# Sandwich block: expert weights loaded from ACT's queue instead of SP's, and a new order of the steps of an expert pair

## The chip, the cores and the metric

One core of a Trainium2 chip runs the whole kernel. TensorE (PE) multiplies matrices into PSUM; VectorE (DVE), ScalarE (ACT) and GpSimd (POOL) do the rest of the arithmetic; SyncE (SP) computes nothing and issues most of the transfers, which 16 DMA engines carry out. Each engine works through its own instructions in order. The metric is the device time of one execution in microseconds; the time of a kernel is the median of its timed runs.

## The reference

Eight sequences of 512 rows of width 256 (4096 rows, f32) go through two parts. Both are normalised and added back to their input.

- Attention: 16 query heads over 4 key and value groups, width 128, with positions added to queries and keys, causal softmax, and an output projection.
- Experts: a gate picks the best 6 of 64 experts for each row. Each expert takes at most 64 rows (`CAP`), in the order of the rows, and computes `silu(x @ w_gate) * (x @ w_up)` with hidden width 176, then `@ w_down`. The results are weighted by the gate's scores and summed. A shared expert of width 352 is computed for every row.

```python
x = x + layernorm(attention(layernorm(x)))
buf  = rows of layernorm(x) gathered by expert       # 64 experts x 64 places x 256
g, u = silu(buf @ w_gate), buf @ w_up                # 256 -> 176
d    = (g * u) @ w_down                              # 176 -> 256
y    = sum over the 6 chosen of topk_w * d  +  shared expert
x = x + layernorm(y)
```

## The kernel before

**Attention sets the beat.** The main loop (lines 884 to 936) runs over `k`, the 128 pairs of a sequence and a head; here such a pass is called a head. The order of the instructions on every engine is written out by hand: what stands first in the loop is issued first. Head `k` computes `scores(k)` (`psc`, line 280; DVE's minimum, line 284; ACT's exponentials, line 287), `project(k-3)` (`po`, line 352), `queries(k+1)` (`pq`, line 267) and `mix(k-2)` (`pav`, line 340, then ACT's copy `ao`, line 108). The probabilities of head `k-1` are turned on the way: DVE transposes blocks into `eb` (line 313), SP stores them to a DRAM tile (`ex_d`, line 317) and loads them back in four parts as `et` (line 320), which `mix` reads one head later. The four loads wait until the store has landed.

**Experts run beside it.** When five sequences have been routed (`EARLY = 5`), the generator `experts()` (lines 612 to 631) works through 32 pairs of experts, two experts of 64 rows side by side. It is advanced at fixed places of the loop, four times in most heads, and each pair step takes two advances; so most heads hold two steps, one in the middle (line 903) and one at the end (line 934). In step `m` stand, for different pairs:

```python
for behind_, step in ((5, down), (4, turn_hidden), (3, gate_up), (2, turn_rows),
                      (1, load_gate_up), (2, load_down)):
    if 0 <= m - behind_ < NM:
        step(m - behind_)
```

- `start_pair` (line 501): POOL gathers the pair's rows into `gx`.
- `load_gate_up` (line 509): two transfers of 352 KB into `wgu`, two buffers. `load_down` (line 518): one of 352 KB into `wd`, two buffers.
- `turn_rows` (line 525): two PE transposes `ptx` (128x128), DVE's copy `gxt`.
- `gate_up` (line 536): PE's `pgu`, for each of the two experts a product with 64 columns of the array (a column-tiled product: the two experts' outputs lie in the two halves of the PSUM tile), then ACT's tanh `hid` (line 544). DVE makes `hid` of it at the next advance (lines 550 and 551).
- `turn_hidden` (line 553): two PE transposes `pth` (128x88), DVE's copy `ht`.
- `down` (line 562): PE's `pd`, column-tiled in the same way, then two ACT activations `dd` (line 576), and POOL's scatter-add into `y_d` (line 577).

A load has to wait until the products of the pair two before have read its buffer. `load_gate_up(m-1)` stands in the step in which `gate_up(m-3)` frees the buffer. `load_down(m-2)` stands one step ahead of `down(m-4)`, which frees its buffer. All these loads are issued by SP, in one queue with `ex_d` and `et`.

PSUM banks come from three pools; `pq`, `pav`, `pd` and `pgu` take turns in three banks (`ps_m`), `psc`, `pth` and `ptx` in three others (`ps_s`).

At the end, pairs with more rows than fit are done again ("late": lines 915 to 923 and the loop from line 948), through the same loading functions with the key `"late"`.

Of the kernel before, what the change touches and what calls it, by code (L numbers as in the profile page):

```python
# [19 lines left out]
P = 128  # L20
# [10 lines left out]
FC = F // 2  # L31
# [12 lines left out]
def sandwich_kernel(ctx, tc, x, wq, bq_t, wkv, bk_t, bv, wo, gate_wt, w_gate, w_up, w_down,  # L44
                    sh_gate_t, sh_up_t, sh_down_t, pe_t, out):
    nc = tc.nc
# [75 lines left out]
    with ExitStack() as part:  # L122
# [313 lines left out]
        def tables():  # L436


            pm = ps_m.tile([NX, CAP], F32, tag="m", name="pm")
            nc.tensor.matmul(pm, lhsT=ident[:, NX:], rhs=keys[0][:, :CAP], start=True, stop=True)  # L440
            both = p1.tile([NX, 2 * CAP], F32, tag="both", name="both")
            nc.vector.tensor_copy(both[:, :CAP], keys[0][:NX, :CAP])
            nc.vector.tensor_copy(both[:, CAP:], pm)
            first = p1.tile([NX, CAP], F32, tag="first", name="first")
            yield
            for n, _ in enumerate(best(first, both)):
                if n % 2:
                    yield
            pk = ps_m.tile([P, NM], F32, tag="m", name="pslot")
            cols = ident[:NX, :NX].rearrange("p (m k) -> p k m", k=2)  # L450
            for odd in range(2):
                nc.tensor.matmul(pk[ts(odd, CAP), :], lhsT=first, rhs=cols[:, odd, :], start=True, stop=True)
            none = p1.tile([P, NM], F32, tag="none", name="none")
            nc.vector.tensor_scalar(none, pk, 0.0, own, ALU.is_equal, ALU.mult)
            row = p1.tile([P, NM], F32, tag="row", name="row")
            nc.vector.tensor_scalar(row, pk, 0.0, float(ET_ROWS - NT), ALU.is_equal, ALU.mult)
            nc.vector.tensor_sub(row, row, pk)
            idx = p1.tile([P, NM, 2], U32, tag="idx", name="idx")
            nc.vector.tensor_scalar_add(idx[:, :, 0], row, float(NT))
            nc.vector.scalar_tensor_tensor(idx[:, :, 1], row, offs, none, ALU.add, ALU.add)  # L460
            table["idx"], table["first"] = idx, first
# [37 lines left out]
        table, pairs = {}, {}  # L499

        def start_pair(m):

            l = pairs[m] = {"m": m}
            l["gx"] = p3.tile([P, ROW], F32, tag="gx", name=f"gx_{m}", bufs=3)
            nc.gpsimd.indirect_dma_start(
                out=l["gx"], out_offset=None, in_=xg_d[:, :],
                in_offset=bass.IndirectOffsetOnAxis(ap=table["idx"][:, m, 0:1], axis=0))

        def load_gate_up(key):
            l = pairs[key]  # L510
            m = l["m"]

            l["wgu"] = p3.tile([P, 2, 2, 2, F], F32, name=f"wgu_{key}", **l.get("wgu_at", {"tag": "wgu"}))
            for k, w in enumerate((w_gate, w_up)):
                nc.sync.dma_start(out=l["wgu"][:, :, k, :, :].rearrange("p e c f -> p e (c f)"),
                                  in_=w[ds(m * 2, 2)].rearrange("e (p c) f -> p e (c f)", p=P))

        def load_down(key):
            l = pairs[key]
            m = l["m"]  # L520
            l["wd"] = p3.tile([FC, 2, 2, E], F32, name=f"wd_{key}", **l.get("wd_at", {"tag": "wd"}))
            nc.sync.dma_start(out=l["wd"].rearrange("p e c h -> p e (c h)"),
                              in_=w_down[ds(m * 2, 2)].rearrange("e (p c) h -> p e (c h)", p=FC))

        def turn_rows(key):
            l = pairs[key]
# [20 lines left out]
        def gate_up_hidden(key):  # L547
            l = pairs[key]
            pgu = l.pop("pgu")
            nc.vector.scalar_tensor_tensor(l["hid"], l["hid"], 1.0, pgu[:, 0, :], ALU.add, ALU.mult)  # L550
            nc.vector.scalar_tensor_tensor(l["hid"], l["hid"], 0.5, pgu[:, 1, :], ALU.mult, ALU.mult)
# [60 lines left out]
        def experts():  # L612


            yield from tables()
            yield
            yield from free_slots()
            yield
            for m in range(NM + 5):
                if m < NM:  # L620
                    start_pair(m)
                for behind_, step in ((5, down), (4, turn_hidden), (3, gate_up), (2, turn_rows),
                                      (1, load_gate_up), (2, load_down)):
                    if 0 <= m - behind_ < NM:
                        step(m - behind_)
                yield
                if 0 <= m - 3 < NM:
                    gate_up_hidden(m - 3)
                if m == NM + 4:
                    pairs["all"] = True  # L630
                yield
# [243 lines left out]
        queries(0)  # L875
        behind, ahead = {}, iter(())
        routed, zeroing = experts(), zeros()
        twice, finishing = False, False
        FIRST_FREE = (EARLY + 1) * NH + 6
# [4 lines left out]
        for k in range(NK):  # L884
# [30 lines left out]
            if k == FIRST_FREE:  # L915

                work = table["work"]
                table["rest"] = nc.values_load(work[0:1, 0:1], min_val=0, max_val=NM - 1)
                table["m"] = nc.values_load(work[0:1, 1:2], (ET.DVE, ET.SP), min_val=0, max_val=NM - 1)
                pairs["late"] = {"m": table["m"], "wgu_at": {"tag": "wgu_late", "bufs": 1},  # L920
                                 "wd_at": {"tag": "wd_late", "bufs": 1}}
                load_gate_up("late")
                load_down("late")
# [24 lines left out]
        with tc.For_i(0, table["rest"], 1) as n:  # L948
            m = nc.values_load(table["work"][0:1, ds(n + 2, 1)], (ET.DVE, ET.SP), min_val=0, max_val=NM - 1)
            pairs["late"] = {"m": m}  # L950
            load_gate_up("late")
            load_down("late")
            parts, gts = [], []
            for b in range(EARLY, B):
                q, tag = [(p1, "hid"), (p2, "v"), (p2, "v")][b - EARLY]
                xg = q.tile([P, NI, LROW], F32, tag=tag, name=f"rest_xg_{b}")
                nc.sync.dma_start(out=xg, in_=rows_of(lxg_d, b * T - ET_ROWS))
                q, tag = [(p1, "y"), (p2, "x"), (p2, "x")][b - EARLY]
                mark, marked = marks(m, xg[:, :, E:ROW], xg[:, :, ROW:], f"rest_{b}", q, tag)
                parts.append((xg, mark))  # L960
                gts.append(turn_scores(marked, f"rest_{b}", p2, "kt", 5))
            gather("late", parts)
            gate_up("late")
            gate_up_hidden("late")
            turn_hidden("late")
            down("late")
            for b in range(EARLY, B):
                y = p2.tile([P, NI, E], F32, tag="xnt", name=f"rest_y_{b}")
                nc.sync.dma_start(out=y, in_=rows_of(ly_d, b * T - ET_ROWS))
                for i in range(NI):  # L970
                    py = ps_m.tile([P, E], F32, tag="m", name=f"rest_py_{b}_{i}")
                    nc.tensor.matmul(py, lhsT=gts[b - EARLY][:, ts(i, P)], rhs=pairs["late"]["dd"], start=True, stop=True)
                    nc.vector.tensor_add(y[:, i, :], y[:, i, :], py)
                nc.sync.dma_start(out=rows_of(ly_d, b * T - ET_ROWS), in_=y)
                for _ in output(b, y, residual(b, p1, "xn")):
                    pass
# [50 lines left out]
```

## Time and profile before

| What | us |
|---|---|
| median of three timed runs | 1498.71 (1498.46 to 1499.84) |
| the profiled execution, its own time | 1494.35 |
| its span, first to last instruction | 1492.6 |
| PE busy in the span | 1416.8 (95%) |
| DVE busy | 891.6 (60%) |
| ACT busy | 498.0 (33%) |
| POOL busy | 427.8 (29%) |
| the stage in which the expert pairs run | about 995 to 1302 |

"Busy" is time in which an engine works on at least one instruction. PE's matmuls are pipelined, so a busy PE can still be held up between two of them. A float32 matrix product shows as two matmul instructions. The clock that the throttle grants to PE is listed for each stretch of time as a share of full speed. "SPq" in a listing is SP issuing a transfer; the duration there is the time for which the issue holds SP, not the transfer. DMA share is the time that packets took, over 16 engines; packets of two queues that overlap are both counted, so it can pass 1.

### The profile page before, as it was taken

What the parts mean: (1) busy time and instruction counts of PE and PEld (TensorE: products, weight loads), DVE (VectorE), ACT (ScalarE), POOL (GpSimd) and SP (SyncE); (2) the same over time, 40 slices, a digit from 0 to 9 for tenths busy, and PEclk for the clock granted to TensorE, in tenths of its full rate; (3) what the DMA queues carried; (4) which work ended last, traced back from release to release, by engine and by line L of the source; (5) the groups of instructions that cost most, each with busy time, mean ns of one, the idle gap of its engine ahead of it and who ended that gap; (6) DMA issues with size and microseconds to landing.
All of it is one profiled execution on the core that took longest, in us unless ns stands there. A gap on an engine that the chain in (4) does not pass through costs nothing.

```text
span 1492.6 us, 18592 instructions
## 1 busy us (share of the span) xinstructions
PE 1416.8 (95%) x5350; PEld 856.4 (57%) x5350; DVE 891.6 (60%) x3094; ACT 498.0 (33%) x1434; POOL 427.8 (29%) x682
## 2 busy tenths in 40 slices
PE   7999999999999999999999999989899999999894
PEld 3566655666656665666566656655455545565552
DVE  4565576657665676557665766666455445577442
ACT  1333343233332342233323332233323333444322
POOL 1222231124112322123112311135333354534202
PEclk9999999999999999999999999999999999999997
DMA  5764554355544464355435544459888799878611
GB/s 207 222 189 142 153 165 139 106 155 166 146 140 134 146 185 125 120 159 165 139 104 165 161 142 132 137 164 258 232 239 230 199 251 261 214 215 249 191 48 60
DMA packets 159701, 252.02 MB, mean 169 GB/s; under 512 B 16092, under 2 KB 135869, under 8 KB 159341
## 3 DMA queue, kind: packets, MB, share of 16 engines
q1 hardware_dynamic: 153453, 241.37, 54.3%
q0 software_dynamic: 6144, 9.44, 3.2%
q8 instruction: 44, 0.72, 0.2%
q14 instruction: 60, 0.49, 0.1%
HBM read 143.01 MB, written 107.74 MB: 168 GB/s over the span
## 4 chain that ended last, share of the span: by engine, by line
PE 79%; DMA 8%; DVE 7%; ACT 2%; POOL 1%; issue 1%; SPq 1%; ACTq 0%; POOLq 0%; DVEq 0%
PE pav L340 16%; PE psc L280 15%; PE pq L267 13%; PE po L352 12%; PE pk L239 4%; PE pv L250 4%; DMA ex_d<-eb 3%; PE py L684 3%; PE pgu L541 3%; PE psg L671 3%; PE psu L671 2%; DVE eb L313 2%; DMA wgu<-in_w_up 2%; PE pd L567 2%; DMA y<-y_d 1%
## 5 line engine op out<-in xcount | busy, mean ns | idle before, releaser
L297 POOL TENSOR_SCALAR e<-e,recip 128x128 f32<-128x128 f32 x508 | 266.5, 542 | 847.4 <-DVE recip L294 809.8
L287 ACT ACTIVATE e<-e,least 128x128 f32<-128x128 f32 (+3 forms) x512 | 285.9, 559 | 379.4 <-DVE least L284 372.1
L280 PE MATMUL psc<-kt,qt 128*128 128x128 f32 (+3 forms) x1024 | 309.6, 442 | 21.0 <-DVE least L284 9.9
L340 PE MATMUL pav<-et,v 128*128 128x512 f32 (+3 forms) x1024 | 296.9, 433 | 2.6 <-DMA et<-ex_d 1.8
L340 PEld LDWEIGHTS pav<-et,v 128*128 128x128 f32 x1024 | 194.4, 190 | 165.3 <-issue 122.8
L284 DVE CUSTOM_DVE_ANT_0 e<-psc,mask 128x128 f32<-128x128 f32 (+3 forms) x512 | 231.3, 479 | 52.3 <-PE psc L280 46.5
L267 PE MATMUL pq<-xnt,wq_sb 128*128 128x512 f32 x512 | 243.9, 599 | 0.0
L352 PE MATMUL po<-wo_sb,ao 128*128 128x256 f32 x1024 | 243.2, 380 | 0.7 <-ACT ao L108 0.7
L352 PEld LDWEIGHTS po<-wo_sb,ao 128*128 128x128 f32 x1024 | 192.5, 190 | 68.6 <-issue 38.2
L313 DVE STREAM_TRANSPOSE eb<-e 128x128 f32<-128x128 f32 x756 | 227.4, 364 | 0.1
L108 ACT COPY ao<-pav 128x512 f32<-128x512 f32 x128 | 75.0, 586 | 450.7 <-PE pav L340 450.7
L280 PEld LDWEIGHTS psc<-kt,qt 128*128 128x128 f32 x1024 | 164.8, 192 | 103.6 <-DVE least L284 34.0
L270 DVE SCALAR_TENSOR_TENSOR qt<-pq,bq_sb,pe_sb 128x512 f32<-128x512 f32 x128 | 95.7, 747 | 121.3 <-PE pq L267 121.2
L267 PEld LDWEIGHTS pq<-xnt,wq_sb 128*128 128x128 f32 x512 | 97.4, 193 | 70.9 <-issue 65.4
L287 ACT ACTIVATION_READ_ACCUMULATOR e<-e,least 128x1 f32 x512 | 95.8, 187 | 0.0
L294 DVE RECIPROCAL recip<-total 128x4 f32<-128x4 f32 x128 | 22.8, 178 | 119.7 <-ACT e L287 119.7
L577 POOL DMA_INDIRECT y_d<-dd,idx x32 | 51.1, 1597 | 72.8 <-ACT dd L576 48.6
L239 PE MATMUL pk<-xnt,wkv_sb 128*128 128x512 f32 x128 | 61.0, 604 | 0.0
L252 DVE TENSOR_TENSOR v<-pv,bv_sb 128x512 f32<-128x512 f32 x32 | 22.1, 692 | 64.4 <-PE pv L250 64.4
L250 PE MATMUL pv<-wkv_sb,xnt 128*128 128x512 f32 x128 | 59.7, 593 | 0.0
L541 PE MATMUL pgu<-wgu,gxt 128*64 128x352 f32 x256 | 47.6, 493 | 10.3 <-DMA wgu<-in_w_up 8.5
L242 DVE SCALAR_TENSOR_TENSOR kt<-pk,bk_sb,pe_sb 128x512 f32<-128x512 f32 x32 | 24.0, 751 | 50.2 <-PE pk L239 50.2
(191 smaller groups left out, 1090.1 us busy)
## 6 DMA issues: line engine op xcount, KB each, us to landing
ex_d<-eb SPq DMA_DIRECT2D x126, 640.0 KB
et<-ex_d SPq DMA_DIRECT2D x504, 160.0 KB
wgu<-in_w_gate SPq DMA_DIRECT2D x32, 352.0 KB
wgu<-in_w_up SPq DMA_DIRECT2D x32, 352.0 KB
wd<-in_w_down SPq DMA_DIRECT2D x32, 352.0 KB
y<-y_d SPq DMA_DIRECT2D x10, 512.0 KB
x<-in_x SPq DMA_DIRECT2D x8, 512.0 KB
x_d<-x SPq DMA_DIRECT2D x8, 512.0 KB
```

The lines of the kernel that those rows point to most:

```text
L239: nc.tensor.matmul(pk, lhsT=wkv_sb[:, c, g, 0, :], rhs=s["xnt"][:, c, :], start=c == 0, stop=c == NC - 1)
L250: nc.tensor.matmul(pv, lhsT=s["xnt"][:, c, ts(i, P)], rhs=wkv_sb[:, c, :, 1, :], start=c == 0, stop=c == NC - 1)
L267: nc.tensor.matmul(pq, lhsT=wq_sb[:, c, ts(h, D)], rhs=seqs[b]["xnt"][:, c, :], start=c == 0, stop=c == NC - 1)
L270: nc.vector.scalar_tensor_tensor(qt, pq, bq_sb[:, h : h + 1], pe_sb, ALU.add, ALU.add)
L280: nc.tensor.matmul(psc[:, :w], lhsT=l["qt"][:, ts(i, P)], rhs=seqs[b]["kt"][h // QPG][:, :w], start=True, stop=True)
L284: nc.vector.tensor_tensor_reduce(out=e, in0=psc[:, :w], in1=mask[:, T - w :], scale=-1.0 / math.sqrt(D), scalar=BIG, op0=ALU.add, op1=ALU. ...
L287: nc.scalar.activation(e, e, AF.Exp, bias=l["least"][:, i : i + 1], scale=-1.0, accum_out=l["total"][:, i : i + 1])
L297: engine.tensor_scalar(e, e, recip[:, n : n + 1], 1.0, ALU.mult, ALU.mult)
L313: nc.vector.transpose(blocks.rearrange("p c j t -> p j c t"), l["e"][i][:, js[0] * P : (js[-1] + 1) * P].rearrange("p (j c t) -> p j c t", ...
L340: nc.tensor.matmul(pav[:, :, j:, :], lhsT=seqs[b]["v"][:, j, ts(g, D)], rhs=l["et"][:, :, AT[j] : AT[j] + NI - j, :], start=j == 0, stop=j ...
L352: nc.tensor.matmul(po[b][i // 2][:, i % 2, :], lhsT=ao[:, ts(i, P)], rhs=wo_sb[:, h, :], start=h == 0 and i % 2 == 0, stop=h == NH - 1, sk ...
L541: nc.tensor.matmul(pgu[ts(e, CAP)], lhsT=l["gxt"][:, c, ts(e, CAP)], rhs=l["wgu"][:, e, :, c, :], start=c == 0, stop=c == 1)
```

## The change

The three weight loads of a pair are issued by ACT instead of SP, except those with the key `"late"`, which stay on SP. In a step, `gate_up` moves ahead of `turn_hidden`, so that the two column-tiled products `pd` and `pgu` follow each other on PE, and the transposes `pth` and `ptx` follow them. `load_down` moves from two steps behind to three, so that it stands behind `down` of the pair two before, whose activations read that pair's result. Since ACT's instructions stay in the order of the program, the loads of a step stand behind that step's `dd` and tanh.

```diff
         def load_gate_up(key):
-            l = pairs[key]
+            l, queue = pairs[key], nc.sync if key == "late" else nc.scalar
             m = l["m"]
 
             l["wgu"] = p3.tile([P, 2, 2, 2, F], F32, name=f"wgu_{key}", **l.get("wgu_at", {"tag": "wgu"}))
             for k, w in enumerate((w_gate, w_up)):
-                nc.sync.dma_start(out=l["wgu"][:, :, k, :, :].rearrange("p e c f -> p e (c f)"),
-                                  in_=w[ds(m * 2, 2)].rearrange("e (p c) f -> p e (c f)", p=P))
+                queue.dma_start(out=l["wgu"][:, :, k, :, :].rearrange("p e c f -> p e (c f)"),
+                                in_=w[ds(m * 2, 2)].rearrange("e (p c) f -> p e (c f)", p=P))
 
         def load_down(key):
-            l = pairs[key]
+            l, queue = pairs[key], nc.sync if key == "late" else nc.scalar
             m = l["m"]
             l["wd"] = p3.tile([FC, 2, 2, E], F32, name=f"wd_{key}", **l.get("wd_at", {"tag": "wd"}))
-            nc.sync.dma_start(out=l["wd"].rearrange("p e c h -> p e (c h)"),
-                              in_=w_down[ds(m * 2, 2)].rearrange("e (p c) h -> p e (c h)", p=FC))
+            queue.dma_start(out=l["wd"].rearrange("p e c h -> p e (c h)"),
+                            in_=w_down[ds(m * 2, 2)].rearrange("e (p c) h -> p e (c h)", p=FC))
...
-                for behind_, step in ((5, down), (4, turn_hidden), (3, gate_up), (2, turn_rows),
-                                      (1, load_gate_up), (2, load_down)):
+                for behind_, step in ((5, down), (3, gate_up), (4, turn_hidden), (2, turn_rows),
+                                      (1, load_gate_up), (3, load_down)):
```

## The prediction

> **What bounds the kernel now.** First the slices of the page: PE, its granted clock, DMA.
>
> ```profile
> PE   7999999999999999999999999989899999999894
> PEclk9999999999999999999999999999999999999997
> DMA  5764554355544464355435544459888799878611
> ```
>
> PE is full nearly everywhere; around the stage of the expert pairs (slices 27 to 35) it dips while DMA jumps from 4 or 5 to 8 and 9. The change touches that stage alone, so I read it by windows.
>
> ```profile
> 995.00:1302.00 307.00, 291.99 (x1315) 161.35 (x1314) 160.63 (x557) 103.27 (x284) 135.68 (x154) 0.97 0.87 235
> 1224.00:1230.00 6.00, 6.00 (x17) 2.77 (x14) 1.83 (x5) 0.32 (x1) 3.41 (x3) 0.72 0.97 307
> ```
>
> Columns: window, length, busy PE, weight loads, DVE, ACT, POOL, clock, DMA share, GB/s. In 307 us PE is idle for 15.0 us, and the clock falls to 0.72 in some windows. PE's waits in the stage:
>
> ```profile
> PE pgu L541 <- DMA wgu<-in_w_up: 8.5, 5, 2.5
> PE ptx L530 <- DVE st_o L76: 2.4, 1, 2.4
> PE pgu L541 <- ACT dd L576: 1.7, 1, 1.7
> ```
>
> The third is a weight wait too: at 1270.2 ACT's `dd` had begun and frees nothing that `pgu` needs, while the `wgu` transfer issued at 1265.62 was 6 us under way, as long as those in the first row took. So weights cost 8.5 + 1.7 = 10.2 us of idle PE. Why are they late? SP's own waits in the stage, then a stretch of the timeline.
>
> ```profile
> SPq L320 <- DMA ex_d<-eb: 121.6, 17, 13.7
> SPq L522 <- PE pd L567: 59.2, 13, 12.6
> ```
>
> ```profile
> 1247.65 1.78 SPq L320 DMA_DIRECT2D et<-ex_d  x4
> ...
> 1249.53 0.39 SPq L515 DMA_DIRECT2D wgu<-in_w_gate  x1
> ...
> 1249.96 0.47 SPq L515 DMA_DIRECT2D wgu<-in_w_up  x1
> ...
> 1254.83 0.32 SPq L522 DMA_DIRECT2D wd<-in_w_down  x1
> ...
> 1255.25 0.35 SPq L317 DMA_DIRECT2D ex_d<-eb  x1
> ...
> 1255.91 1.40 PE L541 MATMUL pgu<-wgu,gxt 128*64 128x352 f32 x8 [0.73 <-DMA wgu<-in_w_up]
> ...
> 1263.35 1.74 SPq L320 DMA_DIRECT2D et<-ex_d  x4
> ```
>
> The mid-head step's weights go out at 1249.53, behind `et`, which waited for the store `ex_d`; their buffer had been free since that step's `pgu` ended at about 1242.3. They are read at 1255.91: 6 us of lead instead of 13. Then `wd` waits for a `pd` and holds back `ex_d` and the next `et`. The queue's order makes the wait, not the buffers.
>
> [...]
>
> **The change, part by part.** Against the profiled execution's 1494.35 us.
>
> *Weight waits.* Loads issued by ACT stand behind the tanh `hid`, which follows the end of the `pgu` that frees the buffer, so the mid-head pair goes out at about 1242.6 instead of 1249.5. At stake: 10.2 us of idle PE, and the slow clock after it. Lost there is window times (1 - clock): from 1044, 6 x 0.26 = 1.6; from 1074, 6 x 0.20 = 1.2 and 6 x 0.08 = 0.5; from 1224 and from 1272, 1.7 each; 6.6 us. Together 16.8. From below nothing comes back if bytes are the limit. The sections that hold these waits (995 to 1090 and 1205 to 1302, 192 us) move 244 and 242 GB/s at a share of 0.89; 23 us shorter they would need 243 x 192/169 = 276 GB/s, and the best 6 us window has 321 (1134 to 1140). That is close, so I take three quarters: 12.6 us.
>
> *Tiling switches.* One step of a pair on PE:
>
> ```profile
> 1115.43 1.08 PE L567 MATMUL pd<-wd,ht 88*64 88x256 f32 x8
> 1116.44 0.46 PE L558 MATMUL pth<-ident,hid 128*88 128x128 f32 x2
> 1116.83 1.40 PE L541 MATMUL pgu<-wgu,gxt 128*64 128x352 f32 x8
> 1118.16 0.51 PE L530 MATMUL ptx<-ident,gx 128*128 128x128 f32 x2
> 1118.51 2.45 PE L280 MATMUL psc<-kt,qt 128*128 128x128 f32 x8
> ```
>
> From `pd` to `pth` are 1.01 us. The other products give 0.84 ns per column (512 columns start 427 ns apart), so `pd`, with two halves of the array at once, streams 4 x 213 ns = 0.85: 0.16 us goes to the switch. `pgu`: 1.33 - 4 x 0.293 = 0.16. `pth` to `pgu`: 0.39 against two transposes, 0.1 to 0.16 over. Today a step switches four times (before `pd`, `pth`, `pgu`, `ptx`), afterwards twice. Two fewer save between 0.16 and 0.3 us; I take 0.2. Steps 5 to 34 hold both products: 30 x 0.2 = 6.0 us, range 3 to 9. PE is what ends the stage, so this counts in full.
>
> *Issues on ACT.* Each step's three take 0.39 + 0.47 + 0.36 us on SP (medians): 1.22; 32 steps, 39 us on ACT, whose busy time in the stage goes from 103 to 142 of 307. Mid-head, ACT next waits 4.1 us for `pav` (`ao`: 73.0 us in 18 waits): hidden. At the head's end it next waits 0.9 us for the minimum of `e`, then 2.2 us before the third `e` (1267 to 1269): hidden as well. Taken as 0; without cover, 39 us.
>
> *ACT's new waits.* The built program makes every transfer wait for one about eight earlier, which used the same completion semaphore. For ACT these are mostly older weights; the second step of a head, however, waits for that head's `ex_d` and its first `et`. Queued behind are the next head's exponentials, whose reciprocal DVE waits for, and DVE's `qt` is what PE needs. A stall is absorbed up to about 5 us: 2.2 before the third `e`, and 2.7 between `dd` (done 1125.2) and the `pav` (1127.9) that takes its bank. In a short head `ex_d` can go at 1252.6 (the end of `eb`) instead of 1255.25, lands by 1260.7 if it takes 8.1 us as today, and its `et` some 3 us later (estimate from its quarter of 640 KB), when ACT is just there (tanh at 1264.4). Value: 0; bounds 0 and +3 us in each of 17 heads.
>
> *SP, and `wd`.* SP loses the 59.2 us of waiting for `pd`, so `ex_d` and `et` go earlier; PE waits for `et` nowhere in the stage, so 0. `wd` waited for the `down` of the next step anyway in 13 of 32 cases; one step later it still has two steps of lead, the same as `wgu`. 0; bounds 0 to +3.
>
> Sum: -12.6 - 6.0 = -18.6, or 1475.8 us of profiled time. The timed median lies 0.3% above this execution, so I scale: 1498.7 x 1475.8/1494.35 = 1480 us.
>
> **Rivals.**
> *Bandwidth keeps the waits.* For: share 0.87 over the stage, and the late loads follow stretches at 1.05 and over. Against: 11% of the time in those sections is free, and the 1074 window moves 142 GB/s while PE starves, so order, not bytes, is to blame there. Then a quarter or less of the 16.8 comes back: -4 - 6 = -10 or less; 1489, from 1486 to 1495.
> *It does not do what it says.* Switches hide under weight loads that wait anyway, and the weight waits only move to the pair behind: within 3 us, 1496 to 1501.
> *Slower: ACT stalls at its issues.* One place, the second step of a head: ACT waits for `et` of that head. It decides once `et` lands more than 5 us after the tanh. A store takes up to 14 us today (SP's longest wait 13.7); with two queues sharing, `et` could land 8 us late: 3 us in 17 heads, +51 - 18.6 = +32; at 7 us late, +15. From 1503 to 1535. Against: the store no longer stands behind 1 to 2 MB of weights in one queue.
>
> **How the numbers follow.** Weights in time 0.57, bandwidth 0.23, no effect 0.06, ACT stalls 0.14. Likeliest 1480, its own range 1473 to 1486. Below 1473 all of both gains (16.8 + 9) is needed. To leave out no more than 2 in 10 the range reaches over the bandwidth case: 1473 to 1497. 0.2%, or 3 us, is about what a measurement of this kernel can tell from no change: faster 0.80, same 0.06, slower 0.14.
>
> **What would show it.** In the stage, PE's rows for `wgu` fall below 3 us and the windows of clock 0.72 go, but for the one at 1002 (after DVE's `st_o`). SP's row for `pd` is gone. From `pd` to what follows `ptx`, 2.9 us instead of 3.1. The stage lasts about 288 us. ACT shows `wgu` and `wd` issues of 0.3 to 0.5 us behind `hid`. I am wrong if ACT's issues take over 1 us, if the first `e` of heads starts over 3 us after its minimum, or if PE waits for `qt` or for banks that `dd` frees.

## The result, and the profile after

| | median of the runs, us | ratio to before, 95% interval |
|---|---|---|
| before | 1498.80 | |
| changed | 1490.76 | 0.9947 (0.9935 to 0.9959) |
| changed, measured again | 1489.30 | 0.9939 (0.9915 to 0.9963) |

The change makes the kernel about 8 us faster (1498.80 - 1490.76), 0.53%. I had forecast 1480, 18.7 us faster. The direction and the wide range were right; the size was not, and the measured time is that of my rival "bandwidth keeps the waits" (1486 to 1495).

The profiled execution of before (1494.35) lies below the median of its runs and the first one of the changed kernel (1494.10) above its own, so the two spans (1492.6 and 1492.3) don't show the gain, and I use a second profile of the changed kernel (1485.00) beside the first.

First the slices of the changed kernel's page: PE, its clock, DMA. They look much as before; in the stage, DMA stands at 8 and 9.

```profile
PE   7999999999999999999999999988899998898894
PEclk9999999999999999999999999999999999999987
DMA  5764554355544464355435544469998899777511
```

The steps of a pair on PE (start, duration; the changed kernel). From `pd` to what follows `ptx` are 1026.77 - 1024.04 = 2.73 us; before, 1118.51 - 1115.43 = 3.08. `pgu` follows `pd` after 0.91 us; before, `pth` followed it after 1.01.

```profile
1024.04 1.08 PE L567 MATMUL pd<-wd,ht 88*64 88x256 f32 x8
1024.95 1.36 PE L541 MATMUL pgu<-wgu,gxt 128*64 128x352 f32 x8
1026.24 0.46 PE L558 MATMUL pth<-ident,hid 128*88 128x128 f32 x2
1026.54 0.40 PE L530 MATMUL ptx<-ident,gx 128*128 128x128 f32 x2
1026.77 1.88 PE L267 MATMUL pq<-xnt,wq_sb 128*128 128x512 f32 x4
```

PE's waits between 980 and 1310 us (total, times, longest), the changed kernel, first profile:

```profile
PE pd L567 <- DMA wd<-in_w_down: 6.5, 2, 4.4
PE psc L280 <- DVE ht L111: 6.0, 2, 4.4
PE pav L340 <- ACT dd L576: 5.0, 4, 2.8
PE ptx L530 <- DVE mv_o L82: 2.8, 1, 2.8
```

The rows for `wgu` (8.5 and 1.7 us before) are gone, as forecast. Three new ones stand in their place, 17.5 us together: `wd`, which is now late; `ht`, whose copy stands behind DVE's wait for the next sequence's `x` (5.97 us, from SP's store and load of `x`); and a bank that ACT's `dd` frees late. SP's and ACT's waits show more ("..." stands for rows left out). SP:

```profile
SPq L320 <- DMA ex_d<-eb: 118.7, 21, 9.3
...
SPq L317 <- DMA et<-ex_d: 18.5, 5, 6.9
...
SPq L143 <- DMA x_d<-x: 8.3, 1, 8.3
```

ACT, same kernel and window:

```profile
ACT dd L576 <- DMA y_d<-dd,idx: 19.2, 6, 6.2
ACT e L287 <- DMA et<-ex_d: 19.0, 8, 5.5
...
ACT ao L108 <- DMA wgu<-in_w_up: 7.8, 2, 4.0
```

SP no longer waits for `pd` (59.2 us before), but the wait for `ex_d` is not much shorter (129.5 us before in the same window). ACT, which waited for no transfer here before, now waits for the scatter-add that still reads `dd` (19.2 us), and stands at some of its weight issues. The longest such stall:

```profile
1239.75 0.58 ACTq L515 DMA_DIRECT2D wgu<-in_w_up  x1
1245.10 0.32 ACTq L522 DMA_DIRECT2D wd<-in_w_down  x1
1245.52 0.40 ACT L287 ACTIVATE e<-e,least 128x128 f32<-128x128 f32 x1 [5.51 <-DMA et<-ex_d]
```

`hid` had ended at 1240.01 and the issue before at 1240.33; the next went out at 1245.10, and `e`, whose minimum had been ready since 1240.68, was queued behind it. In the trace this issue carries the same semaphore (100) as the first part of `et`, issued at 1236.45, whose last piece landed at 1245.07. Pauses of over 0.3 us ahead of a weight issue add up to 15.9 us in seven places of the first profile and 12.4 in the second. The rows of `ao` are no such stalls, although they name transfers: at 1112.16, for one, the issues were out by 1109.20 and `ao` followed the end of its `pav` at 1112.12.

**A ledger for the stage.** I cut each trace from the first `ptx` of the stage to its last `pd` and split the length in three: PE idle (length minus busy time), slow clock (the sum of length x (1 - clock) over windows of 4 us), and the rest, which is PE's work at full speed. For the kernel before, the window is this (columns as in the prediction); 296.36 - 283.78 = 12.6 us are idle.

```profile
1002.54:1298.90 296.36, 283.78 (x1281) 156.29 (x1281) 155.41 (x537) 97.70 (x270) 129.10 (x144) 0.97 0.87 235
```

And for the second profile of the changed kernel:

```profile
1002.01:1288.76 286.75, 272.38 (x1281) 157.98 (x1281) 154.94 (x532) 98.14 (x270) 124.51 (x140) 0.98 0.91 242
```

| | length | idle | slow clock | work |
|---|---|---|---|---|
| before | 296.4 | 12.6 | 8.5 | 275.3 |
| changed, first profile | 292.9 | 19.5 | 6.8 | 266.5 |
| changed, second profile | 286.8 | 14.4 | 5.1 | 267.3 |

PE has 8 to 9 us less work and loses about as much time as before, or more (21.1 us before, 26.3 and 19.5 after). So the new order gave what it could, and the waits did not go: they changed their names. That is what the experiments had to explain. Two profiles of one kernel differ here by 7 us in what is lost, so single profiles are read for work and for names of waits, and the timed runs for sizes.

**How early the loads go out.** The lead of a load is the time from the end of its issue (of the second transfer for `wgu`) to the start of the product that reads it. Over the 32 pairs, in us:

| | `wgu`, median | shortest | `wd`, median | shortest |
|---|---|---|---|---|
| before | 10.6 | 5.2 | 15.4 | 10.4 |
| changed, first profile | 13.9 | 9.9 | 12.3 | 8.4 |
| changed, second profile | 13.5 | 9.9 | 12.1 | 8.4 |

So the change did give `wgu` the lead that I wanted, and took lead from `wd`. Before, five of the six longest waits for `wgu` had leads of 5.5 to 7.2 us: late issues. The longest wait for `wd` in the changed kernel had a lead of 14.5:

```profile
1020.33 0.43 ACTq L522 DMA_DIRECT2D wd<-in_w_down  x1
...
1035.22 1.97 PE L567 MATMUL pd<-wd,ht 88*64 88x256 f32 x8 [4.41 <-DMA wd<-in_w_down]
```

In the kernel before, a `wgu` transfer of the same size, issued at 1023.02, was in time with a lead of 5.2. So this wait comes neither from a late issue nor from the size of a single transfer alone. The DMA share from 1020.33 to 1035.22 is 1.03, but it was 1.04 in the kernel before from 1023.02 to 1028.60, so the share doesn't tell the two transfers apart. What held this one so long isn't shown.

### The profile page after: what moved, and what is told of

Same layout as the page of the kernel before. It is cut to its first block, busy times and chain, and to the rows that moved or that the text cites. A ratio compares the mean times of both kernels' runs of the same rounds, so it can differ in the third digit from the quotient of the medians.

```text
span 1492.3 us, 18593 instructions
## 1 busy us (share of the span) xinstructions
PE 1409.6 (94%) x5350; PEld 860.8 (58%) x5350; DVE 890.7 (60%) x3094; ACT 499.5 (33%) x1434; POOL 427.4 (29%) x682
## 5 line engine op out<-in xcount | busy, mean ns | idle before, releaser
L297 POOL TENSOR_SCALAR e<-e,recip 128x128 f32<-128x128 f32 x508 | 269.6, 570 | 814.5 <-DVE recip L294 781.6
L267 PE MATMUL pq<-xnt,wq_sb 128*128 128x512 f32 x512 | 240.8, 593 | 0.0
L577 POOL DMA_INDIRECT y_d<-dd,idx x32 | 51.0, 1593 | 108.0 <-DMA y_d<-dd,idx 43.3
L111 DVE COPY ht<-pth 88x256 f32<-88x256 f32 x32 | 13.4, 418 | 69.5 <-PE pth L558 69.4
```

The source lines that it names most:

```text
L267: nc.tensor.matmul(pq, lhsT=wq_sb[:, c, ts(h, D)], rhs=seqs[b]["xnt"][:, c, :], start=c == 0, stop=c == NC - 1)
L297: engine.tensor_scalar(e, e, recip[:, n : n + 1], 1.0, ALU.mult, ALU.mult)
```

## The experiments

Two theories. **Bytes**: the 16 DMA engines are so loaded in the stage that something is always late, whichever queue issues it. **ACT's stalls**: the loads come in time, but ACT waits at its issues and holds back exponentials and banks.

### One part of the change at a time

Only the order of the steps (`b_order`), all loads on SP as before:

```diff
-                for behind_, step in ((5, down), (4, turn_hidden), (3, gate_up), (2, turn_rows),
+                for behind_, step in ((5, down), (3, gate_up), (4, turn_hidden), (2, turn_rows),
                                       (1, load_gate_up), (2, load_down)):
```

> The kernel before with one edit: gate_up stands ahead of turn_hidden; all loads stay on SP and load_down stays two steps behind. It measures the tiling switches alone. In the trace after the change a step goes from pd to what follows ptx in 2.73 us instead of 3.08, 0.35 us less, in 30 steps 10.5 us. Full switch saving (both theories, congestion and ACT stalls): 0.35 x 30 = 10 us faster than before, about 1488; the changed kernel's other part is then worth nothing or less. My recorded 0.2 us a step: 6 us faster, 1493. If the saving is hidden under weight waits: under 3 us, 1496 to 1499.

Measured: 1499.31, ratio 0.9999 (0.9980 to 1.0017). Nothing, and that is the sharpest result of the study. Its ledger: length 300.2, idle 24.1, slow 8.5, work 267.6. The work fell by 7.7 us, and the idle time grew by 11.5. PE's waits of this kernel:

```profile
PE pgu L541 <- DMA wgu<-in_w_up: 21.0, 9, 3.8
PE ptx L530 <- DMA gx<-xg_d,idx: 3.1, 1, 3.1
```

`pgu` now starts 0.91 us after `pd` instead of 1.40 where it needn't wait, but its weights come no sooner: 8.5 + 1.7 = 10.2 us of waits became 21.0, and 10.8 us more over 30 steps is 0.36 us a step, most of the 0.49 by which `pgu` had moved forward.

Only the move of the loads (`b_act`): the changed kernel with the old order.

```diff
-                for behind_, step in ((5, down), (3, gate_up), (4, turn_hidden), (2, turn_rows),
+                for behind_, step in ((5, down), (4, turn_hidden), (3, gate_up), (2, turn_rows),
                                       (1, load_gate_up), (3, load_down)):
```

> The changed kernel with the old order of steps (turn_hidden ahead of gate_up): ACT issues the loads and load_down stands three steps behind. It measures the move of the loads alone. As predicted (12.6 us of weight waits come back): 1486. Congestion (transfers only land later): 1496 to 1499. ACT stalls (the trace shows some 42 us of ACT waiting for et, x or older weights at its issues): 1499 to 1504, with ACT's waits for et and y_d as in the changed kernel.

Measured: 1492.76, ratio 0.9961 (0.9949 to 0.9974): 6.0 us faster than before, half of my 12.6, and between the cases that I had written down. Work 275.4, idle 11.8, slow 5.1. So the new order adds only 1492.76 - 1490.76 = 2.0 us on top of it (the intervals of `b_act` and of the changed kernel overlap).

Only `load_down` one step later, on SP (`b_down3`); and that with the new order (`b_sp`), which is the changed kernel with its loads back on SP.

```diff
-                                      (1, load_gate_up), (2, load_down)):
+                                      (1, load_gate_up), (3, load_down)):
```

> The kernel before with one edit: load_down three steps behind instead of two, still on SP. It takes away SP's 59 us of waiting for pd without touching ACT. If the queue's order made the weight waits, ex_d and et and the next wgu go earlier and part of the 10.2 us of waits for wgu goes: 1492 to 1496. If bytes make them: 1497 to 1500, and the waits for wgu stay near 10 us. wd could come late, since it is loaded a step later: then PE waits for wd appear and the time is 1500 to 1503.

> The changed kernel with the loads on SP as before: the new order of steps and load_down three steps behind. Against the changed kernel (1491) it tells what the other queue is worth. If ACT's stalls eat the gain, this one is as fast or faster: 1485 to 1490. If the earlier loads on ACT are worth what I forecast, it is slower: 1493 to 1498. If bytes decide, it is the same as the changed kernel within 2 us.

Measured: 1496.10, ratio 0.9988 (0.9975 to 1.0001), and 1492.51, ratio 0.9953 (0.9930 to 0.9975). In `b_down3` the waits for `wgu` fall to 0.4 us, and this takes their place:

```profile
PE pd L567 <- DMA wd<-in_w_down: 13.9, 7, 4.4
```

With SP's wait for `pd` gone, `wgu` is in time, and `wd`, issued a step later (median lead 11.6 us instead of 15.4), is late instead. And `b_sp` reaches nearly the whole gain without ACT's queue: of about 8 us, some 6 come without moving a load to another engine (the intervals of `b_sp` and of the changed kernel overlap). The order alone gave nothing, but behind the later `load_down` it gives 1496.10 - 1492.51 = 3.6 us (those two intervals just touch).

### Half the bytes

Both kernels with transfers of one expert instead of two, `wd` in the same way as `wgu`. The number, order and shape of the instructions stay; what the kernels leave out is the second expert's weights, so that expert is computed with the first one's.

```diff
-                queue.dma_start(out=l["wgu"][:, :, k, :, :].rearrange("p e c f -> p e (c f)"),
-                                in_=w[ds(m * 2, 2)].rearrange("e (p c) f -> p e (c f)", p=P))
+                queue.dma_start(out=l["wgu"][:, 0:1, k, :, :].rearrange("p e c f -> p e (c f)"),
+                                in_=w[ds(m * 2, 1)].rearrange("e (p c) f -> p e (c f)", p=P))
...
-                                     rhs=l["wgu"][:, e, :, c, :], start=c == 0, stop=c == 1)
+                                     rhs=l["wgu"][:, 0, :, c, :], start=c == 0, stop=c == 1)
```

> The changed kernel with half the weight bytes: each transfer brings one expert of the pair only, and the products of both experts read it, so the second expert of a pair is computed with the first one's weights. The number of transfers, products and waits stays. Congestion: the stage moves 17 of some 70 MB less, the waits for wd go from 6.5 us to near 0, dd waits less for y_d, and the time falls to 1474 to 1482 (the switches' 8.8 us and the forecast's waits come back). ACT's waits for completion semaphores alone (they hang on the order, not on bytes): 1487 to 1491, with ACT's waits for et as long as before.

> The kernel before with half the weight bytes, in the same way (the second expert of a pair computed with the first one's weights). Congestion: its waits for wgu (10.2 us) go, and so does the slow clock after them: 1484 to 1489; the changed kernel with half the bytes then lies 8 to 10 us below it, the whole saving of the switches. If SP's order alone made the waits, as the prediction has it: the waits for wgu stay over 6 us, 1493 to 1498.

Measured: the changed kernel with half the bytes 1468.21, ratio 0.9801 (0.9772 to 0.9830); the kernel before with half the bytes 1473.11, ratio 0.9833 (0.9803 to 0.9862); before, measured beside them, 1497.44. The stage's windows, before with half the bytes:

```profile
1000.72:1278.65 277.93, 275.61 (x1280) 152.12 (x1280) 157.56 (x540) 97.61 (x270) 130.17 (x146) 1.00 0.70 188
```

The changed kernel with half the bytes:

```profile
1000.63:1271.01 270.38, 267.23 (x1280) 155.20 (x1281) 158.29 (x540) 98.45 (x270) 130.64 (x146) 1.00 0.74 193
```

Read the clock (1.00 in both) and the idle time: 277.93 - 275.61 = 2.3 us and 270.38 - 267.23 = 3.2 us. With nothing else lost, the busy time is the work: 275.6 against 267.2, so the new order, in which PE changes between column-tiled products and others twice a step instead of four times, is worth 8.4 us in 30 steps, 0.28 us a step. That these changes make it, and not the order in another way, stays my estimate, since no run takes out a change alone: of the 0.35 us in the steps shown, 0.10 lie between `pd` and its successor, 0.09 behind `pth`, 0.04 behind `pgu`, and 0.12 behind `ptx`, where no such change stands in either order. DMA share went from 0.87 and 0.91 to 0.70 and 0.74.

Three things follow. The bytes cost the kernel before 1497.44 - 1473.11 = 24.3 us, more than the 16.8 I saw in its one profile, of an execution 4 us below the median. They cost the changed kernel 1490.76 - 1468.21 = 22.6 us, or 21 to 22 by the two ratios to the kernel before measured beside it: of about 24 us the change gave back 2 to 4. And SP's order alone doesn't make the waits. In the half-byte kernel before, SP still waits for `pd`, longer than ever, and PE waits for no weight at all:

```profile
SPq L522 <- PE pd L567: 91.3, 22, 12.7
SPq L320 <- DMA ex_d<-eb: 87.0, 23, 5.8
```

`wgu` goes out hardly earlier there: 11 of the 32 leads are under 9 us (13 before), the shortest 4.2. But the wait for `ex_d` is shorter (129.5 us before, longest 13.7), and each weight transfer has 176 KB instead of 352. So this pair of runs shows that the bytes make the waits; it doesn't tell the load of all engines from the size of the late transfers. For the changed kernel the lead of 14.5 us above tells only that the issue wasn't late.

In the changed kernel with half the bytes ACT's stalls are gone with the waits: no weight issue is held up by over 0.3 us (15.9 us in all with full bytes). So it can't weigh them against the bytes; it shows that the stalls hang on the bytes too. What speaks against ACT's stalls as the main cause is that the kernel before and `b_order`, `b_down3` and `b_sp`, which have no such loads on ACT, lose as much: 21 to 33 us of idle time and slow clock.

### Which queue, and which wait

Only the mid-head steps' loads on ACT (odd pairs, from the fifth on), the others on SP:

```diff
-            l, queue = pairs[key], nc.sync if key == "late" else nc.scalar
+            l, queue = pairs[key], nc.scalar if key != "late" and key % 2 else nc.sync
```

> The changed kernel, but only the mid-head steps' loads are on ACT; the loads of the step at a head's end go back to SP, in the same place. ACT then never waits at the end of a head for that head's ex_d or et (19 + 6 us in the changed kernel's trace). ACT stalls: 1483 to 1488, the waits for dd and ht of 11 us shrink. Congestion: 1489 to 1493, the same as the changed kernel.

> The changed kernel with only the mid-head steps' loads on ACT, once more, since its first interval (0.9897 to 0.9952) still touches that of the changed kernel. If ACT's stalls at the end of a head cost time, it is faster than the changed kernel of the same call by 3 to 6 us: 1484 to 1487. If its first result was chance: 1489 to 1491.

Measured: 1484.61, ratio 0.9924 (0.9897 to 0.9952), and once more 1486.24, ratio 0.9906 (0.9885 to 0.9927): the fastest kernel of the study, 3 to 6 us below the changed one (1489.30, measured beside the second run), though the intervals of each pair still touch. ACT's rows for `et` are gone, and no weight issue is held up by over 0.4 us. PE's waits, second profile:

```profile
PE pd L567 <- DMA wd<-in_w_down: 11.6, 4, 8.4
PE pav L340 <- ACT dd L576: 4.4, 4, 2.1
```

Still 26.5 us lost in this profile and 19.1 in the first; the work is 266 to 267.

The mirror, only the loads at a head's end on ACT (`a_end`: `key % 2 == 0` in the line above):

> The mirror of the last: only the loads of the step at a head's end are on ACT, those of the mid-head step are on SP, behind et. If the waits of ACT for ex_d and et at a head's end cost the time, this kernel has them all and loses the earlier mid-head loads as well: 1492 to 1497. If it is only that fewer bytes in ACT's queue leave more for SP's and POOL's, it is like the kernel with the mid-head loads: 1484 to 1487.

Measured: 1497.01, ratio 0.9975 (0.9958 to 0.9992), 10.8 us slower than the kernel with the mid-head loads. As the ACT theory had it in number, but not in kind. This is all that ACT waits for `et`:

```profile
ACT e L287 <- DMA et<-ex_d: 4.1, 2, 2.6
```

And this is what PE waits for `wd` in the same kernel:

```profile
PE pd L567 <- DMA wd<-in_w_down: 16.9, 5, 5.2
```

ACT hardly stalls in it (1.6 us at its issues); `wd` is late. With all loads on SP as the starting point (1492.51), moving the mid-head loads gains 6.3 to 7.9 us in medians, 4 to 7 by the ratios to the kernel before measured beside each, and moving those of the head's end costs 4.5 in medians, 3.3 by the ratios (the intervals of `a_end` and `b_sp` overlap, and so do those of `a_mid` and `b_sp`; those of `a_mid_2` and `b_sp` just don't). The first is the part of my forecast that held. Why the second costs isn't settled: ACT's stalls are too short in `a_end`, and `b_sp` waits for `wd` nearly as long, 15.6 us.

Three buffers for `dd` (`a_dd3`), which takes away the wait of `dd` for the scatter-add of two pairs ago:

```diff
-            dd = p3.tile([P, E], F32, tag="dd", name=f"dd_{key}")
+            dd = p3.tile([P, E], F32, tag="dd", name=f"dd_{key}", bufs=3)
```

> The changed kernel with three buffers for dd instead of two. dd then waits for the scatter-add of three pairs ago. If the wait of dd for y_d (19.2 us on ACT, and through it 5.0 us of PE waiting for a bank) costs the time: 1485 to 1488. If ACT's other stalls or the bytes do: 1489 to 1492, and only that row of waits goes.

Measured: 1489.92, ratio 0.9942 (0.9923 to 0.9960): no difference. The row of `pav` waiting for `dd` shrinks from 5.0 us to 0.3, and in the same profile:

```profile
PE psc L280 <- DVE ht L111: 14.3, 2, 9.9
PE pd L567 <- DMA wd<-in_w_down: 5.9, 4, 2.1
```

One more wait taken away, one more that grew instead.

The old order with the mid-head loads on ACT (`b_mid`):

> The kernel with the mid-head loads on ACT, but in the old order of steps. It tells what the order is worth once the loads come well. Work in the stage should be 275 us instead of 267. If bytes limit, the old order only waits less and the time is within 3 us of the kernel with the new order: 1485 to 1489. If the order now pays in full: 8 us more, 1491 to 1495.

Measured: 1490.84, ratio 0.9938 (0.9918 to 0.9957), 4.6 us above its twin with the new order (1486.24, measured beside it; the intervals overlap). Work 274.6 against 266 to 267. So the order pays 4.6 of its 8.4 us here, 2.0 with all loads on ACT, 3.6 on SP with `load_down` a step later, and nothing on SP with `load_down` where it was. The first three are not told apart by these runs.

The changed kernel again, measured beside these:

> The changed kernel once more, for a second profile and for times beside the next three. Its first profile lay above its median. Expected: a ratio of 0.995 again, 1490, with waits of PE for wd, dd and ht of 10 to 18 us in all; the windows between the first ptx and the last pd hold about 267 us of time in which PE neither idles nor runs slow, and 20 to 26 us of idle and slow clock.

Measured: 1489.30, as in the table at the top; lost 19.5 us, a little under what I had expected from one profile. Its named waits are 12.2 us for `ht`, `dd` and `wd`.

### A peak, or the whole stage?

In every kernel with full bytes, one of the largest waits lies between 1024 and 1078 us, where steps become two a head and the next sequence's `x` is stored and loaded. These kernels take the second step out of heads 101 and 102 (or 99 to 102), from the kernel before and from the one with the mid-head loads on ACT:

```diff
-            if twice and not finishing:
+            if twice and not finishing and k not in (101, 102):
                 next(routed, None)
```

> The kernel before, but heads 101 and 102 hold one pair step instead of two; the steps left out come later, so that the stage ends one head later with the same work. If a peak of transfers there makes the waits of 1045 to 1080 us (5.6 us of waits for wgu and some 3 us of slow clock): 1491 to 1494. If the stage is short of bandwidth throughout, the waits only move on: 1496 to 1500. The end of the kernel has one head less for finishing the early sequences, which could cost 0 to 2 us in either case.

> The changed kernel with only the mid-head steps' loads on ACT, and with one pair step instead of two in heads 101 and 102. Peak: the wait of 5.2 to 8.4 us for wd at 1052 to 1057 and the slow clock behind it (3.4 us) go: 1478 to 1481 against 1485 without it. Average load: 1484 to 1487, with as much waiting elsewhere.

> As the last, but heads 99 to 102 hold one pair step each, so that the stage ends two heads later. If the peak is all: the same as with two heads, 1478 to 1481, or a little above if the end has too few heads left. If relief goes on: 1475 to 1478. Average load: 1483 to 1486.

Measured: 1512.31, ratio 1.0076 (1.0047 to 1.0106); 1491.31, 0.9956 (0.9940 to 0.9973); 1499.49, 1.0001 (0.9981 to 1.0021). All are slower than without the edit. In `a_skip2` the wait at 1052 to 1057 fell from 5.2 or 8.4 us for `wd` to 1.62 for DVE's minimum, but one of 4.53 us for `dd` appeared at 1275. PE's waits of `b_skip2`, between 980 and 1325 us:

```profile
PE pgu L541 <- DMA wgu<-in_w_up: 10.5, 5, 3.0
PE psc L280 <- DVE least L284: 5.9, 2, 4.6
PE pt_f L118 <- DVE least L284: 4.2, 1, 4.2
```

The waits for `wgu` are what they were (8.5 + 1.7 us), four of the five now between 1244 and 1295. That speaks for the load of the whole stage. But the edit adds a cost of its own, since a head without its second step leaves PE idle for DVE's minima (4.2 and 4.6 us), and the end of the kernel has one head less. So the three runs refute the gain that I expected, and tell peak from stage only in part.

## Why the prediction was wrong, step by step

- **Weight waits, -12.6: the step that failed.** It took three quarters of 16.8 us back because "the queue's order makes the wait, not the buffers". The half that was right: before, `wgu` went out late (leads of 5.5 to 7.2 us at five of six waits), and the change gave it at least 9.9. What failed is the step from an earlier issue to a shorter wait. Measured alone, the move of the loads gave 6.0 us (`b_act`), part of which comes from `load_down` (2.7 us in `b_down3`, not certain: the interval reaches 1.0001). The waits hang on the bytes: these cost 24.3 us before and 21 to 22.6 after, and in the changed kernel `wd`, which lost 3 us of lead, was late once after 14.5 us. Against my step stood, in my own text, 276 GB/s needed and a share of 0.89. What I took for proof, a window of 142 GB/s while PE starved, was one window; the load that PE waited for there had been out for 12 us, through windows with shares of 1.09 and 1.01.
- **Tiling switches, -6.0.** The saving of work was there and larger: 0.28 us a step instead of 0.2, 8.4 us in all, inside my 3 to 9. My 0.16 us for one switch was an estimate, 1.01 us from `pd` to `pth` less 0.85 of columns; in the step shown, `pd`'s successor came 0.10 us sooner. "PE is what ends the stage, so this counts in full" failed: it counted 0.0 with `b_order`, 2.0 with all loads on ACT, 3.6 in `b_sp`, 4.6 with the mid-head loads on ACT. In `b_order` the work taken from PE became waiting of PE. With half the bytes, where PE hardly waits, it counted 4.9 in the medians of six runs each and 7.7 between the two profiled executions (1473.25 - 1465.51); the runs don't settle which.
- **ACT's issues, 0.** Their lengths came as forecast: the three have medians of 0.38, 0.48 and 0.40 us. What they cost was not measured alone. ACT's busy time, which I expected to rise from 103 to 142 us in the stage, can't show it, since issues don't count as busy there (499.5 us in all, 498.0 before).
- **ACT's new waits, 0, bounds to +51.** They came, 15.9 us at the weight issues, and `dd` waited 19.2 us for the scatter-add, which I had not listed. Loads of the head's end on ACT cost 3 to 6 us of the kernel's time (changed against `a_mid`, where ACT doesn't stall; the intervals touch). I should have put 3 to 6 where I put 0; the rival of +32 was far off.
- **SP and `wd`, 0.** Wrong in kind: `wd` was late in every kernel with full bytes and `load_down` three steps behind (13.9 us in `b_down3`, 6.5 and 2.3 in the changed one). My reason, that it has as much lead as `wgu`, left out that it is the last of three transfers and is read by `down`, the first product of a step: median leads of 12.3 us against 13.9, and 15.4 before the change.
- **The signs I named.** The rows for `wgu`, SP's row for `pd` and the 2.9 us (2.73) came as written. The stage shrank by 3.5 and 9.6 us in the two profiles, not by the 19 I had written, and the slow clock stayed (6.8 and 5.1 us of 8.5). Two signs of being wrong came: PE waited for a bank that `dd` frees, and a first `e` started over 3 us after its minimum (1240.68 to 1245.52).

The rival "bandwidth keeps the waits" had the cause, the bytes, and the time, and should have been the likeliest: the sections' share of 0.89 was its evidence. That its 1489 was met so well is partly luck. It put 4 us on the loads and 6 on the switches; measured one after the other they gave 6.0 and 2.0.

Issuing the loads from a second engine hardly changed the rate in the stage: 235 GB/s before, 237 and 242 after. Yet moving the mid-head loads off SP gained 4 to 8 us. On SP these loads stand behind `et`, whose issue waits for `ex_d` for up to 11.5 us in `b_sp`.

## What to carry over

Before pricing a better order of loads, halve their bytes and look: if the waits go although the loads go out no earlier, the bytes have a part in them. Then take the lead of each late load: a short one speaks for the order, one as long as the 14.5 us here against a late issue. Here a wait that was taken away came back under another name: in `a_dd3` the wait for `dd` went from 5.0 to 0.3 us and that for `ht` from 6.0 to 14.3. With full bytes the 8.4 us of work saved on PE were worth 0.0 to 4.6 us here. On ACT's queue the mid-head loads gained 4 to 7 us by the ratios, those at the head's end cost 3.3, and the kernel with only the first on ACT was the fastest, 1484.61 to 1486.24.

## What the runs showed that I had not expected

- The scatter-add got into the way. By the listing, POOL waited 3.8 us in the stage for its previous scatter-add in the kernel before and up to 15.8 in the others with all loads on SP, but 43.3 us in the changed kernel (57.1 in `b_act`). It goes with the mid-head loads on ACT and with their bytes. ACT's `dd`, which waits for an earlier scatter-add too, waited 19.2 and 20.6 us for it in the changed kernel's two profiles and 18.2 and 21.8 with the mid-head loads alone on ACT; with only those of the head's end ACT's listing has no such row down to 4.1 us, and in the changed kernel with half the bytes none down to 0.3. The scatter-add's median time to land went only from 6.7 to 7.4 us. How the two get into each other's way isn't shown.
- The slow clock comes mostly in pieces of 1.7 us: 8.5, 6.8, 5.1 and 3.4 us of loss in the ledgers. In the stage of the kernel before, the clock is 0.50 in five stretches of 3.41 us, from 1002.45, 1046.82, 1077.54, 1224.32 and 1272.10; in that of the changed kernel's first profile it is 0.50 for 6.83 us from 1033.68 and for 3.41 us from 1060.99 and from 1255.55. A wait as short as 1.7 us (until 1271.90) was followed by one in the kernel before, but one of 2.77 us in the changed kernel (until 1284.50) was not: the clock stayed 1.00 to 1288.50. So the length of a wait alone doesn't tell whether a slow stretch follows it; what does isn't shown.
- A sequence's `x`, whose load waits until the store of another sequence has landed, was late only where the mid-head loads went to ACT: with full bytes SP waited 6.3 to 8.3 us there for that store, and 1.6 to 3.3 us with those loads on SP.
